# Putting an attention pass between the chunks of a product, layernorms on ScalarE, and a second PSUM bank: a four-layer graph network on one core

## The chip, the cores and the metric

The kernel runs on one core of one Trainium2 chip. The metric is device time in microseconds (us), median of the runs. TensorE is PE in the profiles, VectorE DVE, ScalarE ACT, GpSimd POOL. A "product" below is one matmul call; in fp32 it leaves two instruction records in the trace, so x64 in a profile are 32 calls. A "chunk" is a 1 MB piece of adj or of its transpose as it is loaded, a "block" a group of 512 nodes, a "bank" one of the parts of PSUM, the memory that TensorE writes its sums to.

## The reference, cut to what matters

Four graph layers on N = 4096 nodes with 128 features, each `x = layernorm(x + layer(x))`, all with one 4096 x 4096 matrix `adj`. The change touches the end of the second, the third and the fourth:

```python
# second layer: two Chebyshev convolutions (K = 3) with elu; its last step is one product of adj
# with a 4096 x 128 matrix ("w" below), elu, layernorm
# third layer: attention, 4 heads of 32
C = alpha_src[None, :, :] + alpha_dst[:, None, :]
tau = adj.T[..., None] * exp(maximum(0.2 * C, C))
att = tau / sum(tau, axis=1, keepdims=True)
z = einsum('mnh,nhf->mhf', adj.T[..., None] * att, h_prime)
# fourth layer
out = h @ W_self + (adj @ h / deg) @ W_neigh
```

## The kernel before

The third layer runs in 8 passes (1024 target nodes and 2 of 4 heads each) of 32 steps (128 source nodes each). A step is a vector job with a small product at its end: DVE forms tau, POOL and DVE multiply it once more by the matrix, PE multiplies both into two PSUM banks, `den` and `num`, with 32-column weights.

```python
def attention(mp, hp, between):
    ...
    for nt in range(NT):
        ...                                             # a: chunk of adj; sq = a*a on ScalarE
        for h in range(2):
            nc.vector.scalar_tensor_tensor(tau[:, h, :], D[h], E(h), a, op0=ALU.max, op1=ALU.mult)
        nc.vector.scalar_tensor_tensor(tau2[:, 0, 0:OWN], D[0][:, 0:OWN], E(0), sq, ...)
        nc.gpsimd.tensor_tensor(tau2[:, 0, OWN:WB], tau[:, 0, OWN:WB], a[:, OWN:WB], ALU.mult)
        nc.gpsimd.tensor_tensor(tau2[:, 1, :], tau[:, 1, :], a, ALU.mult)
        product(den, nt, tau, True)
        ...                                             # product(num, ...) of the step before
        between()                                       # one product of the fourth layer
```

After each second pass two blocks of x are complete: their layernorm and the fourth layer's weights follow ("layer-4 block"), and the fourth layer's product with adj runs in pieces in the next two passes ("left-over product"; its last quarter is all that runs after pass 8). Before all this stands the last product of the second layer, whose blocks feed the passes:

```python
for ib, blk, p in propagate(lambda jt: w[:, jt, :], extra=extra):   # 8 blocks of 32 products + wd @ hT, the part that needs no adj
    oT = l1w.tile([P, IB], F32, name="t2T")
    elu(oT, p, B1B)
    ...                                            # transpose, add to x, layernorm
    sources_and_targets(ib)                        # scores: cs, es, hc (sources), dv (targets)
...
def layer3_product(mp):                            # the left-over product
    for ib in range(NB):
        ...
        if mp == 0:
            nc.scalar.copy(acc3[:, blk], p)
        else:
            nc.vector.tensor_add(acc3[:, blk], p, acc3[:, blk])
```

## Time and profile before

Median 2413.23 us (four runs, 2413.23 to 2418.12); the profiled run's span is 2412.5.

| stage | us |
|---|---|
| second layer, last product but one ("v") | 241 |
| second layer, last product | 254 |
| from its end to pass 1 | 20 |
| pass 1, pass 2 | 105, 107 |
| pass 3, pass 4 | 141, 110 |
| pass 5, 6, 7, 8 | 119, 110, 121, 109 |
| left-over product after pass 8 | 94 |

Second part of the profile page, three of its lines: busy share in tenths in 40 equal slices of the span, about 60 us each.

```profile
PE   4899999999999999999999878889888999999987
...
DVE  4433458776011010000222299998799999899965
...
POOL 0000000000000000000000089988798899799940
```

Digits 11 to 23 (most of the second layer) are 8 or 9 on PE and 0 to 2 on DVE; from digit 24 DVE and POOL are busy. Work of the second kind could lie beside work of the first: that is the intent of the change. Its windows by stage stand in the prediction.

### The profile page before, as it was taken

How to read it: one execution, taken by the hardware profiler on the slowest of the kernel's cores; microseconds unless marked ns; L12 is line 12 of the kernel's file. 1: busy time of each engine (PE TensorE's matmuls, PEld its weight loads, DVE VectorE, ACT ScalarE, POOL GpSimd, SP SyncE). 2: the span in 40 equal slices, each digit the busy share in tenths (PEclk: the TensorE clock that was granted, in tenths of full speed). 3: DMA queues.
4: the chain of work that ended last, by engine and by line, in shares of the span. 5: the costliest groups of instructions: out<-in, count | busy, mean ns of one | idle time of the engine just before them, and what ended most of it. 6: DMA issues, size and time to landing. Idle time of an engine off the chain costs nothing. (4 is left out here: it accounts for less than half of the span.)

```text
span 2412.5 us, 23257 instructions
## 1 busy us (share of the span) xinstructions
PE 2252.8 (93%) x8798; PEld 863.4 (36%) x8798; DVE 1366.3 (57%) x2011; ACT 463.3 (19%) x660; POOL 840.4 (35%) x542
## 2 busy tenths in 40 slices
PE   4899999999999999999999878889888999999987
PEld 2334444444444444444444411112222222222233
DVE  4433458776011010000222299998799999899965
ACT  5665000000000000000111122222222222222210
POOL 0000000000000000000000089988798899799940
PEclk8899999999999999999999989999999999999999
DMA  9988788999877878888888735546665666566655
GB/s 361 347 277 261 244 244 259 294 293 291 265 234 244 263 238 278 277 277 276 261 266 264 244 120 160 157 140 209 209 207 194 210 215 239 192 226 232 228 178 168
DMA packets 261802, 575.39 MB, mean 239 GB/s; under 512 B 9776, under 2 KB 15920, under 8 KB 261680
## 3 DMA queue, kind: packets, MB, share of 16 engines
q1 hardware_dynamic: 252352, 566.27, 72.8%
q10 hardware_dynamic: 9328, 7.54, 1.0%
q8 instruction: 71, 1.16, 0.2%
q14 instruction: 51, 0.42, 0.0%
HBM read 571.67 MB, written 2.10 MB: 238 GB/s over the span
## 5 line engine op out<-in xcount | busy, mean ns | idle before, releaser
L624 DVE SCALAR_TENSOR_TENSOR tau<-d,es,chunk 128x1024 f32<-128x1024 f32 x512 | 632.8, 1275 | 28.8 <-issue 18.4
L628 POOL TENSOR_TENSOR tau<-tau,chunk 128x1024 f32<-128x1024 f32 x256 | 606.3, 2368 | 39.0 <-DVE tau L624 31.7
L608 PE MATMUL num<-tau,hc 128*32 128x512 f32 x2048 | 448.1, 602 | 44.6 <-POOL tau L628 42.7
L557 POOL TENSOR_TENSOR x<-x,B2R 128x512 f32<-128x512 f32 x8 | 10.1, 1268 | 1375.8 <-PE ptr L104 1375.8
L608 PE MATMUL den<-tau,cs 128*32 128x512 f32 x2048 | 482.7, 604 | 6.6 <-DVE tau L624 6.1
L619 ACT ACTIVATE sq<-chunk 128x704 f32<-128x704 f32 x256 | 201.8, 792 | 571.3 <-DVE tau L625 568.2
L676 PE MATMUL pp<-chunk,xT 128*128 128x512 f32 x512 | 270.9, 631 | 18.1 <-DMA chunk<-in_adjT 17.2
L313 PE MATMUL pacc<-chunk,hw 128*128 128x512 f32 x512 | 254.6, 635 | 3.0 <-DVE hw L346 3.0
L627 POOL TENSOR_TENSOR tau<-tau,chunk 128x320 f32<-128x320 f32 x256 | 222.2, 868 | 66.0 <-DVE tau L624 20.9
L625 DVE SCALAR_TENSOR_TENSOR tau<-d,es,sq 128x704 f32<-128x704 f32 x256 | 241.0, 941 | 6.3 <-PE num L608 2.5
L444 PE MATMUL pacc<-chunk,w 128*128 128x512 f32 x512 | 226.7, 592 | 0.0
L444 PE MATMUL pacc<-chunk,t 128*128 128x512 f32 x512 | 223.6, 592 | 0.0
L444 PE MATMUL pacc<-chunk,x 128*128 128x512 f32 x512 | 223.5, 594 | 0.0
L444 PE MATMUL pacc<-chunk,v 128*128 128x512 f32 x512 | 221.4, 592 | 0.0
L608 PEld LDWEIGHTS num<-tau,hc 128*32 128x32 f32 x2048 | 83.6, 108 | 291.3 <-POOL tau L628 126.2
L608 PEld LDWEIGHTS den<-tau,cs 128*32 128x32 f32 x2048 | 93.0, 108 | 212.9 <-DVE tau L624 98.8
L293 DVE TENSOR_SCALAR pos<-chunk 128x2048 bf16<-128x2048 f32 x92 | 110.7, 1221 | 75.0 <-DMA chunk<-in_adjT 70.7
L676 PEld LDWEIGHTS pp<-chunk,xT 128*128 128x128 f32 x512 | 82.2, 189 | 198.4 <-issue 165.3
L444 PEld LDWEIGHTS pacc<-chunk,v 128*128 128x128 f32 x512 | 96.6, 190 | 118.1 <-issue 118.1
L444 PEld LDWEIGHTS pacc<-chunk,t 128*128 128x128 f32 x512 | 96.1, 190 | 114.8 <-issue 114.8
L444 PEld LDWEIGHTS pacc<-chunk,x 128*128 128x128 f32 x512 | 95.9, 190 | 113.9 <-issue 113.8
L444 PEld LDWEIGHTS pacc<-chunk,w 128*128 128x128 f32 x512 | 94.9, 190 | 110.3 <-issue 110.3
(161 smaller groups left out, 1321.4 us busy)
## 6 DMA issues: line engine op xcount, KB each, us to landing
chunk<-in_adjT SPq DMA_DIRECT2D x412, 1024.0 KB, 5.5
chunk<-in_adj SPq DMA_DIRECT2D x128, 1024.0 KB, 5.4
xT<-in_xT ACTq DMA_DIRECT2D x8, 256.0 KB, 6.6
out<-o ACTq DMA_DIRECT2D x8, 256.0 KB, 4.0
W1A<-in_w1a ACTq DMA_DIRECT2D x1, 384.0 KB, 8.0
W1B<-in_w1b ACTq DMA_DIRECT2D x1, 384.0 KB, 9.9
W0T<-in_w0gT ACTq DMA_DIRECT2D x1, 64.0 KB, 4.3
W<-in_w0g ACTq DMA_DIRECT2D x1, 64.0 KB, 7.1
```

What stands on the lines that cost most here:

```text
L293: nc.vector.tensor_scalar(pos, a, 0.0, None, op0=ALU.is_gt)
L313: nc.tensor.matmul(p, hw[:, j * TB + k, :], a[:, k, :], start=first and k == 0, stop=last and k == TB - 1)
L444: nc.tensor.matmul(p, stationary(c * TB + k), a[:, k, :], start=n == 0 and k == 0, stop=n == NB - 1 and k == TB - 1 and not more)
L557: nc.gpsimd.tensor_tensor(x[:, tb, :], x[:, tb, :], B2R[:, None, :].to_broadcast([P, TB, F]), ALU.add)
L608: nc.tensor.matmul(acc[q:q + 32, :], weights(nt, 2 * hp + h, is_den), r[:, h, mb * IB:(mb + 1) * IB], start=nt == 0, stop=nt == NT - 1)
L619: nc.scalar.activation(sq, a[:, 0:OWN], AF.Square)
L624: nc.vector.scalar_tensor_tensor(tau[:, h, :], D[h], E(h), a, op0=ALU.max, op1=ALU.mult)
L625: nc.vector.scalar_tensor_tensor(tau2[:, 0, 0:OWN], D[0][:, 0:OWN], E(0), sq, op0=ALU.max, op1=ALU.mult)
L627: nc.gpsimd.tensor_tensor(tau2[:, 0, OWN:WB], tau[:, 0, OWN:WB], a[:, OWN:WB], ALU.mult)
L628: nc.gpsimd.tensor_tensor(tau2[:, 1, :], tau[:, 1, :], a, ALU.mult)
L676: nc.tensor.matmul(p, y[:, (2 * mp + c) * TB + k, :], a[:, k, :], start=c == 0 and k == 0, stop=c == 1 and k == TB - 1)
```

## The change

Four parts. (1) The product of wd with hT leaves the last product for the one before it, and the result (h0T) is added back by VectorE; this frees hT's memory. (2) Pass 1 becomes a generator, and 28 of its 32 steps are issued between the chunks of the last product (6, 5, 5, 4, 4, 4 in blocks 2 to 7), 4 after it. (3) The layer-4 layernorm is done by ScalarE and the residual goes into its weight matrix (+ identity), so that ScalarE copies it. (4) In the last quarter of the left-over product, blocks alternate between two PSUM banks. Core of the diff, cuts marked:

```diff
+    nc.gpsimd.tensor_tensor(W3[:, 1, :], W3[:, 1, :], ident, ALU.add)
...
+            if on_act:
+                nc.scalar.activation(r[:, k, :], r[:, k, :], AF.Identity, bias=m[:, k:k + 1], scale=s[:, k:k + 1])
...
-                    nc.vector.tensor_add(x[:, two, :], q[:, :, 1, :], x[:, two, :])
+                    nc.scalar.copy(x[:, two, :], q[:, :, 1, :])
...
-                    p = ps_p.tile([P, IB], F32, name="pp")
+                    last = mp == NW - 1
+                    p = (ps_nd.tile([P, IB], F32, name="num") if last and ib % 2 else ps_p.tile([P, IB], F32, name="pp"))
...
+                first_pass = attention(l2a, 2, 0, 0)
+                ready = done = 0
+                for ib in range(NB):
+                    p = ps_p.tile([P, IB], F32, name="pp")
+                    for c in range(NB):
+                        a = chunk(ld, adjT, ib, c)
+                        ...                                       # 4 products
+                        if ib >= 2 and done < ready and (c % 2 or ready - done > TB):
+                            next(first_pass)
+                            done += 1
+                    oT = l1w.tile([P, IB], F32, name="t2T")
+                    nc.vector.tensor_add(oT, p, h0T[:, blk])
+                    elu(oT, oT, B1B)
+                    ...
+                    ready += TB
+                for _ in first_pass:
+                    pass
```

Smaller parts: W1A and W1B are loaded later, the squares have two buffers instead of three, and in the last pass x is added on VectorE.

More of the change, by code (lines that the diff above doesn't have):

```diff
@@ L66, in adj_resnorm_d4 @@
         nc.scalar.dma_start(xT[:, g * IB:(g + 1) * IB], xT_in[:, g * IB:(g + 1) * IB])
-    W1A = load_const(w1a.rearrange("k p f -> p k f"), [P, 3, HID], "W1A")
     B1A = load_const(b1a, [P, HH], "B1A")
-    W1B = load_const(w1b.rearrange("k (h p) f -> p (k h) f", p=P), [P, 3 * HH, F], "W1B")
     B1B = load_const(b1b, [P, 1], "B1B")
@@ L110, in stats, with normalize @@
         nc.vector.bn_aggr(mv[:, t, :], st)
-    def normalize(r, g):
+    def normalize(r, g, on_act=False):
+        tb = slice(g * TB, (g + 1) * TB)
         s = small.tile([P, TB], F32, name="rstd")
-        nc.vector.tensor_scalar_add(s, mv[:, g * TB:(g + 1) * TB, 1], LN_EPS)
+        nc.vector.tensor_scalar_add(s, mv[:, tb, 1], LN_EPS)
         nc.scalar.activation(s, s, AF.Sqrt)
         nc.vector.reciprocal(s, s)
+        if on_act:
+            m = small.tile([P, TB], F32, name="mean")
+            nc.vector.scalar_tensor_tensor(m, mv[:, tb, 0], -1.0, s, op0=ALU.mult, op1=ALU.mult)
         for k in range(TB):
-            nc.vector.tensor_scalar(r[:, k, :], r[:, k, :], mv[:, g * TB + k, 0:1], s[:, k:k + 1],
-                                    op0=ALU.subtract, op1=ALU.mult)
+            if on_act:
+                nc.scalar.activation(r[:, k, :], r[:, k, :], AF.Identity, bias=m[:, k:k + 1], scale=s[:, k:k + 1])
+            else:
+                nc.vector.tensor_scalar(r[:, k, :], r[:, k, :], mv[:, g * TB + k, 0:1], s[:, k:k + 1],
+                                        op0=ALU.subtract, op1=ALU.mult)
     def normalize_x(g, pool, name):
@@ L411, in network @@
             l1_pools = ExitStack()
-            with ExitStack() as first:
+            with ExitStack() as first, ExitStack() as l1h_pool:
                 ps_acc, ps_tr, ps_mm = [first.enter_context(tc.tile_pool(name=n, bufs=2, space=PSUM, reuse_waits="tile"))
@@ L421, in network @@
                 dv = state.tile([96, N], BF16, name="dv")
+                selD = state.tile([96, H, P], BF16, name="selD")
                 l1 = l1_pools.enter_context(tc.tile_pool(name="l1", bufs=1, reuse_waits="tile"))
                 l1w = l1_pools.enter_context(tc.tile_pool(name="l1w", bufs=2, reuse_waits="tile"))
+                l1h = l1h_pool.enter_context(tc.tile_pool(name="l1h", bufs=1, reuse_waits="tile"))
+                W1A = l1h.tile([P, 3, HID], F32, name="W1A")
+                nc.scalar.dma_start(W1A, w1a.rearrange("k p f -> p k f"))
+                W1B = l1h.tile([P, 3 * HH, F], F32, name="W1B")
+                nc.scalar.dma_start(W1B, w1b.rearrange("k (h p) f -> p (k h) f", p=P))
                 def elu(dst, p, bias):
@@ L431, in elu, with propagate @@
                     nc.vector.scalar_tensor_tensor(dst, n, -1.0, r, op0=ALU.add, op1=ALU.add)
-                def propagate(stationary, order=range(NB), look=None, extra=None):
+                def propagate(stationary, order=range(NB), look=None):
                     for ib in range(NB):
                         p = ps_acc.tile([P, IB], F32, name="pacc")
-                        more = extra(ib) if extra else []
                         for n, c in enumerate(order):
@@ L444, in propagate @@
                                 nc.tensor.matmul(p, stationary(c * TB + k), a[:, k, :], start=n == 0 and k == 0,
-                                                 stop=n == NB - 1 and k == TB - 1 and not more)
-                        for n, (wgt, r) in enumerate(more):
-                            nc.tensor.matmul(p, wgt, r, start=False, stop=n == len(more) - 1)
+                                                 stop=n == NB - 1 and k == TB - 1)
                         yield ib, slice(ib * IB, (ib + 1) * IB), p
                 t1 = state.tile([P, NT, F], F32, name="t1", tag="yn")
-                t1T = l1.tile([P, N], F32, name="t1T")
-                hT = l1.tile([P, HH, N], F32, name="hT")
-                wd = l1.tile([P, HH, F], F32, name="wd")
+                t1T = l1.tile([P, N], F32, name="t1T", tag="t1T")
+                hT = l1h.tile([P, HH, N], F32, name="hT")
+                wd = l1h.tile([P, HH, F], F32, name="wd")
                 nc.vector.tensor_sub(wd, W1B[:, 0:HH, :], W1B[:, 2 * HH:3 * HH, :])
-                w2x = l1.tile([P, HH, F], F32, name="w2x")
+                w2x = l1h.tile([P, HH, F], F32, name="w2x")
                 nc.vector.tensor_scalar_mul(w2x, W1B[:, 2 * HH:3 * HH, :], 2.0)
-                dsum = l1.tile([P, IB], F32, name="dsum")
+                dsum = l1h.tile([P, IB], F32, name="dsum")
                 def degree(a, first_one):
-                    s = l1w.tile([P, 2, IB], F32, name="dhalf", bufs=1)
+                    s = l1h.tile([P, 2, IB], F32, name="dhalf")
                     nc.vector.tensor_add(s, a[:, 0:2, :], a[:, 2:4, :])
@@ L497, in network @@
                 w = state.tile([P, NT, F], F32, name="w", tag="yn")
+                h0T = l1.tile([P, N], F32, name="h0T", tag="t1T")
                 for ib, blk, p in propagate(lambda jt: v[:, jt, :]):
@@ L507, in network @@
                     nc.vector.tensor_copy(w[:, ib * TB:(ib + 1) * TB, :], q)
-                hc = state.tile([P, NT, H, FO], F32, name="hc", tag="v")
-                att = l1.tile([P, 2, H], F32, name="att")
-                nc.vector.memset(att, 0.0)
-                for h in range(H):
-                    hp = slice(h * FO, (h + 1) * FO)
-                    nc.vector.tensor_copy(att[hp, 0, h:h + 1], ATS[hp, :])
-                    nc.vector.tensor_copy(att[hp, 1, h:h + 1], ATD[hp, :])
-                WD = l1.tile([P, 96], F32, name="WD")
@@ L523, in network @@
-                nc.vector.memset(WD, 0.0)
-                pw = ps_mm.tile([P, 2, H], F32, name="pmm")
-                nc.tensor.matmul(pw, W2, att.rearrange("p s h -> p (s h)"), start=True, stop=True)
-                nc.vector.tensor_copy(W2S[:, F:F + H], pw[:, 0, :])
-                for part in range(3):
-                    nc.vector.tensor_copy(WD[:, 32 * part:32 * part + H], pw[:, 1, :])
-                def sources_and_targets(ib):
-                    blk = slice(ib * IB, (ib + 1) * IB)
-                    for half in range(2):
-                        two = slice(ib * TB + 2 * half, ib * TB + 2 * half + 2)
-                        pn = ps_mm.tile([P, 2, F + H], F32, name="pmm")
-                        for k in range(2):
-                            t = ib * TB + 2 * half + k
-                            nc.tensor.matmul(pn[:, k, :], xT[:, t * P:(t + 1) * P], W2S, start=True, stop=True)
-                        nc.scalar.activation(cs[:, two, :], pn[:, :, F:F + H], AF.Exp, scale=0.2)
-                        nc.scalar.activation(es[:, two, :], pn[:, :, F:F + H], AF.Exp, scale=0.8)
-                        for k in range(2):
-                            t = ib * TB + 2 * half + k
-                            nc.vector.tensor_mul(hc[:, t], pn[:, k, 0:F].rearrange("p (h f) -> p h f", f=FO),
-                                                 cs[:, t, :][:, :, None].to_broadcast([P, H, FO]))
-                    pd = ps_mm.tile([96, IB], F32, name="pmm")
-                    nc.tensor.matmul(pd, WD, xT[:, blk], start=True, stop=True)
-                    d = l1w.tile([96, IB], F32, name="elu_r")
-                    nc.scalar.activation(d, pd, AF.Exp, scale=-0.8)
-                    nc.vector.tensor_copy(dv[:, blk], d)
-                    nc.vector.tensor_sub(d, d, dv[:, blk])
-                    nc.vector.tensor_copy(dv[32:64, blk], d[32:64, :])
-                    nc.vector.tensor_copy(dv[64:96, blk], d[64:96, :])
-                    nc.vector.tensor_sub(d[64:96, :], d[64:96, :], dv[64:96, blk])
-                    nc.vector.tensor_copy(dv[64:96, blk], d[64:96, :])
-                    tb = slice(ib * TB, (ib + 1) * TB)
-                    nc.gpsimd.tensor_tensor(x[:, tb, :], x[:, tb, :], B2R[:, None, :].to_broadcast([P, TB, F]), ALU.add)
@@ L559, in network @@
-                extra = lambda ib: [(wd[:, hh, :], hT[:, hh, ib * IB:(ib + 1) * IB]) for hh in range(HH)]
-                for ib, blk, p in propagate(lambda jt: w[:, jt, :], extra=extra):
-                    oT = l1w.tile([P, IB], F32, name="t2T")
-                    elu(oT, p, B1B)
-                    q = transpose4(ps_tr, "ptr", lambda k: oT[:, k * P:(k + 1) * P])
-                    xb = x[:, ib * TB:(ib + 1) * TB, :]
-                    nc.vector.tensor_add(xb, q, xb)
-                    for t in range(ib * TB, (ib + 1) * TB):
-                        stats(x[:, t, :], t)
-                    normalize_x(ib, ps_tr, "ptr")
-                    sources_and_targets(ib)
@@ L570, in network @@
-            l1_pools.close()
+                    ph = ps_mm.tile([P, IB], F32, name="pmm")
+                    for hh in range(HH):
+                        nc.tensor.matmul(ph, wd[:, hh, :], hT[:, hh, blk], start=hh == 0, stop=hh == HH - 1)
+                    nc.scalar.copy(h0T[:, blk], ph)
             ps_d = enter(name="ps_d", bufs=1, space=PSUM)
@@ L579, in network @@
             ps_x = enter(name="ps_x", bufs=1, space=PSUM)
-            l2w = enter(name="l2w", bufs=1)
-            selD = l2w.tile([96, H, P], BF16, name="selD")
-            rows = l2w.tile([96, H], F32, name="rows")
+            hc = state.tile([P, NT, H, FO], F32, name="hc", tag="v")
+            y = xT.rearrange("p (t f) -> p t f", f=F)
+            att = l1.tile([P, 2, H], F32, name="att")
+            nc.vector.memset(att, 0.0)
+            for h in range(H):
+                hp = slice(h * FO, (h + 1) * FO)
+                nc.vector.tensor_copy(att[hp, 0, h:h + 1], ATS[hp, :])
+                nc.vector.tensor_copy(att[hp, 1, h:h + 1], ATD[hp, :])
@@ L583, in network @@
+            WD = l1.tile([P, 96], F32, name="WD")
+            nc.vector.memset(WD, 0.0)
+            pw = ps_x.tile([P, 2, H], F32, name="px")
+            nc.tensor.matmul(pw, W2, att.rearrange("p s h -> p (s h)"), start=True, stop=True)
+            nc.vector.tensor_copy(W2S[:, F:F + H], pw[:, 0, :])
+            for part in range(3):
+                nc.vector.tensor_copy(WD[:, 32 * part:32 * part + H], pw[:, 1, :])
+            rows = small.tile([96, H], F32, name="rows")
             nc.vector.tensor_reduce(rows, ident[0:96, :].rearrange("p (q c) -> p c q", q=4)[:, 0:H, 0:3], AX.X, ALU.add)
@@ L584, in network, with sources_and_targets @@
             nc.vector.tensor_copy(selD, rows[:, :, None].to_broadcast([96, H, P]))
-            acc3 = state.tile([P, N], F32, name="acc3", tag="yn")
-            y = xT.rearrange("p (t f) -> p t f", f=F)
+            def sources_and_targets(ib):
+                blk = slice(ib * IB, (ib + 1) * IB)
+                for half in range(2):
+                    two = slice(ib * TB + 2 * half, ib * TB + 2 * half + 2)
+                    pn = ps_x.tile([P, 2, F + H], F32, name="px")
+                    for k in range(2):
+                        t = ib * TB + 2 * half + k
+                        nc.tensor.matmul(pn[:, k, :], xT[:, t * P:(t + 1) * P], W2S, start=True, stop=True)
+                    nc.scalar.activation(cs[:, two, :], pn[:, :, F:F + H], AF.Exp, scale=0.2)
+                    nc.scalar.activation(es[:, two, :], pn[:, :, F:F + H], AF.Exp, scale=0.8)
+                    for k in range(2):
+                        t = ib * TB + 2 * half + k
+                        nc.vector.tensor_mul(hc[:, t], pn[:, k, 0:F].rearrange("p (h f) -> p h f", f=FO),
+                                             cs[:, t, :][:, :, None].to_broadcast([P, H, FO]))
+                pd = ps_x.tile([96, IB], F32, name="px")
+                nc.tensor.matmul(pd, WD, xT[:, blk], start=True, stop=True)
+                d = l1w.tile([96, IB], F32, name="elu_r")
+                nc.scalar.activation(d, pd, AF.Exp, scale=-0.8)
+                nc.vector.tensor_copy(dv[:, blk], d)
+                nc.vector.tensor_sub(d, d, dv[:, blk])
+                nc.vector.tensor_copy(dv[32:64, blk], d[32:64, :])
+                nc.vector.tensor_copy(dv[64:96, blk], d[64:96, :])
+                nc.vector.tensor_sub(d[64:96, :], d[64:96, :], dv[64:96, blk])
+                nc.vector.tensor_copy(dv[64:96, blk], d[64:96, :])
+                tb = slice(ib * TB, (ib + 1) * TB)
+                nc.gpsimd.tensor_tensor(x[:, tb, :], x[:, tb, :], B2R[:, None, :].to_broadcast([P, TB, F]), ALU.add)
@@ L588, in weights, with attention @@
             def weights(nt, head, den):
                 return cs[:, nt, head:head + 1].to_broadcast([P, FO]) if den else hc[:, nt, head, :]
-            def attention(mp, hp, between):
+            def attention(l2w, bufs, mp, hp):
                 D = []
@@ L617, in attention @@
                     a = a2t[:, nt % 2, :]
-                    sq = l2w.tile([P, OWN], F32, name="sq", bufs=3)
+                    sq = l2w.tile([P, OWN], F32, name="sq", bufs=2)
                     nc.scalar.activation(sq, a[:, 0:OWN], AF.Square)
-                    tau = l2w.tile([P, 2, WB], F32, name="tau", bufs=3)
-                    tau2 = l2w.tile([P, 2, WB], F32, name="tau2", bufs=3)
+                    tau = l2w.tile([P, 2, WB], F32, name="tau", bufs=bufs)
+                    tau2 = l2w.tile([P, 2, WB], F32, name="tau2", bufs=bufs)
                     E = lambda h: es[:, nt, 2 * hp + h:2 * hp + h + 1]
@@ L632, in attention @@
                         product(num, *late.pop(0), False)
-                    between()
+                    yield
                 product(num, *late.pop(0), False)
@@ L647, in attention @@
                     xb = xb.rearrange("p k (h f) -> p k h f", f=FO)
-                    nc.gpsimd.tensor_tensor(xb, z[:, :, :, mb, :], xb, ALU.add)
+                    eng = nc.vector if mp == NW - 1 and hp == 1 else nc.gpsimd
+                    eng.tensor_tensor(xb, z[:, :, :, mb, :], xb, ALU.add)
             def layer3_block(j):
@@ L654, in layer3_block @@
                     stats(x[:, t, :], t)
-                normalize(x[:, tb, :], j)
+                normalize(x[:, tb, :], j, on_act=True)
                 q = transpose4(ps_x, "px", lambda k: x[:, j * TB + k, :])
@@ L685, in layer3_product @@
                         nc.vector.tensor_add(acc3[:, blk], p, acc3[:, blk])
-                    if mp == NW - 1:
+                    if last:
                         layer3_out(ib)
@@ L699, in layer3_out @@
                 nc.scalar.dma_start(out[ib * IB:(ib + 1) * IB, :].rearrange("(k p) f -> p k f", p=P), o)
+            with tc.tile_pool(name="l2a", bufs=1, reuse_waits="tile") as l2a:
+                first_pass = attention(l2a, 2, 0, 0)
+                ready = done = 0
+                for ib in range(NB):
+                    blk = slice(ib * IB, (ib + 1) * IB)
+                    tb = slice(ib * TB, (ib + 1) * TB)
+                    p = ps_p.tile([P, IB], F32, name="pp")
+                    for c in range(NB):
+                        a = chunk(ld, adjT, ib, c)
+                        for k in range(TB):
+                            nc.tensor.matmul(p, w[:, c * TB + k, :], a[:, k, :], start=c == 0 and k == 0,
+                                             stop=c == NB - 1 and k == TB - 1)
+                        if ib >= 2 and done < ready and (c % 2 or ready - done > TB):
[4 more added lines that the diff above has]
+                    elu(oT, oT, B1B)
+                    q = transpose4(ps_x, "px", lambda k: oT[:, k * P:(k + 1) * P])
+                    nc.vector.tensor_add(x[:, tb, :], q, x[:, tb, :])
+                    for t in range(ib * TB, (ib + 1) * TB):
+                        stats(x[:, t, :], t)
+                    normalize_x(ib, ps_x, "px")
+                    sources_and_targets(ib)
+                    ready += TB
+                for _ in first_pass:
+                    pass
+            l1_pools.close()
+            l2w = enter(name="l2w", bufs=1)
+            acc3 = state.tile([P, N], F32, name="acc3", tag="yn")
             pieces = iter(())
@@ L703, in network @@
                 for hp in range(H // 2):
-                    attention(mp, hp, lambda: next(pieces, None))
+                    if (mp, hp) != (0, 0):
+                        for _ in attention(l2w, 3, mp, hp):
+                            next(pieces, None)
                 for _ in pieces:
```

## The prediction

> **What bounds the kernel now.** I read the stage windows first, then the page's groups, then the chain of waits. The windows (stretch, then busy us per engine, granted clock, DMA share, GB/s) cut the part that the change touches at its stage ends: the second layer's last product, its tail, the eight passes of the third layer, the left-over product.
>
> ```profile
> core 0: us, PE busy (x) PEld busy (x) DVE busy (x) ACT busy (x) POOL busy (x), PEclk, DMA share, GB/s
> 1122.00:1376.60 254.60, 254.60 (x695) 119.01 (x694) 62.31 (x194) 40.16 (x78) 8.87 (x7) 1.00 0.86 266
> 1376.60:1395.30 18.70, 7.04 (x21) 3.55 (x19) 9.43 (x29) 7.80 (x14) 1.27 (x1) 0.63 0.20 67
> 1395.30:1500.60 105.30, 88.65 (x509) 16.84 (x510) 103.83 (x96) 24.58 (x32) 101.08 (x64) 0.97 0.48 150
> 1500.60:1607.30 106.70, 89.14 (x525) 17.13 (x524) 104.78 (x98) 26.36 (x34) 103.59 (x67) 1.00 0.51 158
> 1607.30:1748.30 141.00, 127.37 (x627) 32.89 (x627) 114.72 (x130) 31.98 (x48) 104.44 (x67) 0.98 0.57 194
> 1858.10:1977.40 119.30, 114.56 (x613) 30.80 (x612) 114.19 (x134) 29.25 (x42) 103.89 (x67) 1.00 0.60 206
> 1977.40:2087.80 110.40, 107.97 (x589) 27.09 (x590) 107.57 (x103) 26.45 (x35) 104.01 (x67) 1.00 0.67 229
> 2087.80:2208.90 121.10, 116.36 (x613) 31.25 (x612) 113.72 (x135) 29.33 (x43) 104.07 (x67) 0.99 0.60 208
> 2344.00:2402.00 58.00, 52.67 (x140) 23.44 (x140) 30.68 (x134) 1.44 (x7) 0.00 (x0) 1.00 0.61 195
> ```
>
> The last product is PE's alone: 254.60 of 254.60 us, DVE a quarter busy. The first pass is the reverse: DVE 103.83 of 105.30, POOL 101.08 close behind. So the two stages want different engines, and that is the idea. Pass 3 is 35 us longer than pass 1, passes 5 and 7 some 10 us longer than 6.
>
> ```profile
> L624 DVE SCALAR_TENSOR_TENSOR tau<-d,es,chunk 128x1024 f32<-128x1024 f32 x512 | 632.8, 1275 | 28.8 <-issue 18.4
> L625 DVE SCALAR_TENSOR_TENSOR tau<-d,es,sq 128x704 f32<-128x704 f32 x256 | 241.0, 941 | 6.3 <-PE num L608 2.5
> L628 POOL TENSOR_TENSOR tau<-tau,chunk 128x1024 f32<-128x1024 f32 x256 | 606.3, 2368 | 39.0 <-DVE tau L624 31.7
> L608 PE MATMUL num<-tau,hc 128*32 128x512 f32 x2048 | 448.1, 602 | 44.6 <-POOL tau L628 42.7
> L608 PE MATMUL den<-tau,cs 128*32 128x512 f32 x2048 | 482.7, 604 | 6.6 <-DVE tau L624 6.1
> L444 PE MATMUL pacc<-chunk,w 128*128 128x512 f32 x512 | 226.7, 592 | 0.0
> ```
>
> A step (256 in all, 32 a pass) is two L624 and one L625; in the timeline of passes 1 and 2 the steps follow each other every 3.24 us, and 32 x 3.24 = 104. POOL's two instructions take 2.37 + 0.87 = 3.24 as well.
>
> From the chain of waits (start, us, what):
>
> ```profile
> 1677.82 5.31 DMA chunk<-in_adjT
> 1691.32 5.75 DMA chunk<-in_adjT
> ...
> 1952.65 1.92 PE pp L676 x4
> 1955.56 1.06 PE pp L676 x2
> ...
> 2378.36 6.88 PE pp L676 x16
> 2386.66 6.88 PE pp L676 x16
> ```
>
> Late in pass 3 (and into 4) whole chunk loads lie on the chain, one every 13 to 15 us: the timeline shows 12 of them going in turn into one and the same buffer, each waiting for the last chunk's final matmul. In the left-over product a block is 6.88 us of matmul, but the next begins 8.31 later: 1.43 us for emptying the one PSUM bank.
>
> **What the Trainium skill says.** "TensorEngine Tiling (Array Packing)", Key Properties: changing the tiling mode drains TensorE. The trace agrees: 16 equal products take 6.88 (0.86 a pair), a lone pair between 32-column products 1.06, so 0.20 a switch. "Perfetto Trace Analysis", Identifying the Most-Contended Engine: matmul busy share misleads, as matmuls are pipelined. Agrees: pass 6 shows PE 107.97 of 110.40, yet DVE's 107.57 sets the pace, and PE's weight loads are 27. "VectorE: DVE Perf Modes", Side-by-side: fp32 two-tensor operations get no faster mode; L624's 1275 ns for 1024 elements agrees, so nothing shrinks DVE's step. "ScalarE: Activation LUTs", What ACT_TABLE_LOAD costs: an ACTIVATE is about 280 ns plus 0.83 per element, about 93 more for each pointer operand. My estimate for the moved normalise is then 0.28 + 128 x 0.83 ns + 0.09, near 0.45 us, as dear as on DVE; no instruction of this kind is in the trace.
>
> **The change part by part.**
>
> 1. The product of wd with hT (a pair per call and block, 8 x 1.71 = 13.7 us of PE at 0.857 a call pair) moves from the last product into the one before it, also PE-bound: +13.7 there, -13.7 here, plus one 0.7 us add per block on DVE, idle there.
>
> 2. The interleave. In the changed program's order of instructions, 28 of the 32 steps stand in the last product: 6, 5, 5, 4, 4, 4 in blocks 2 to 7, and 4 after it. What a step costs PE: a group of 4 narrow products alone advances PE 0.98 us, 4 den and 4 num together 1.85 (from starts in the timeline of pass 8, 2276.17 to 2278.02), plus 0.20 for the switch: 2.05. So PE's sum is 254.6 - 13.7 + 28 x 2.05 = 298.3. DVE has 28 x 3.24 + 62 = 153 and POOL about 100 of those 298: no longer bounds. To this I add stalls by judgement: 1.4 us in each of blocks 0 and 1 (the bank is single now; from the third block on, the order puts steps' products ahead of the transposes, which hides it), 3.6, 3.7, 2.6 in blocks 2 to 4 and 2.5 in each of the last three, where a step's products wait for POOL in PE's queue: 20. The stage becomes 318. After it: the block's chain of elu, layernorm and scores 11.7 (of 18.7 today), 4 steps 13, the last quotient 3, some 1 for starting pass 2: 28.7. Together 347. Today the same is 254.6 + 18.7 + 105.3 + 0.5 = 379.1. Gain 32, less part 1's 13.7: **-18.3**. So 94 us of pass hidden cost 57 of PE and 20 of stalls.
>
> 3. Weights W1A and W1B are no longer loaded at the start, which is bound by DMA (768 KB near 380 GB/s: -2), but late in layer 0, where the second layer's first vector work waits for them: +3. **+1**.
>
> 4. Pass 2 has two buffers fewer for the squares and new ones for tau: **+1**.
>
> 5. Layernorms on ScalarE. For a pair of blocks DVE loses 8 x 0.445 (L119 in pass 5) = 3.6, 4 adds of 0.42 = 1.7, and 1.5 of waits for ACT: 6.8 us, at DVE's price because the pass is DVE's. ACT has 75 us spare per pass, but its squares (one a step) stand in the same queue behind the chain, so I count two thirds: -4.5 for each of passes 5 and 7: **-9**. In pass 3 the same, and the order has 10 loads in a row into one buffer in place of 12: **-8** for passes 3 and 4.
>
> 6. Two banks in the left-over product: 7 gaps of 1.43, of which about 1.0 goes (the narrow transposes stay between blocks), and 1 for the x add of the last pass on DVE: **-8**.
>
> Sum: -18.3 + 1 + 1 - 9 - 8 - 8 = -41.3; 2413.2 - 41.3 = 2371.9.
>
> **The rivals.**
>
> A. TensorE becomes the bound and gives the hidden time back. PE executes in order, and a den or num that waits for DVE or POOL holds up the product's matmuls behind it. For it: L608 waits for POOL already, 42.7 us in all; each of blocks 2 to 7 would lose 5 us more, and with the four steps after the end slower, the gain of part 2 goes: near 2400. Against it: products run one step late, and in the merged stage DVE and POOL have twice the time per step.
>
> B. Chunk loads set the pace of passes 3 and 4 whatever DVE does. For it: the DMA lines above, each load 5.3 to 5.8 us. Then part 5's -8 is 0, or worse where the ring of buffers falls otherwise; ScalarE's chain may also delay the squares, as there are 2 buffers for them. 2380 to 2390.
>
> C. The stalls of part 2 are smaller than my 20 us. For it: PE's busy time is modelled, DVE and POOL are far from full, and the order hides the evacuations. With 5 us of stalls and part 5 in full: near 2345.
>
> D. The merged stage becomes DMA's. Against it: 266 GB/s today; 64 chunks plus 14 MB in 318 us are about 256 GB/s. I give it no weight.
>
> **Range and chances.** The one large judged term is the stalls (20, could be 5 to 35), then the passes (-17, could be -25 to 0). Rival A and B together reach 2400, C 2345. Predicted 2372, 8 in 10 between 2348 and 2397. Faster by over 2% needs under 2365: 0.36. Within 2%: 0.62. Slower by 2% needs over 2461: no sum comes near; 0.02.
>
> **What would show it.** Part 2: the stretch from the last product's start to pass 2's first step 347 us with PE over 95% busy up to the product's end; blocks 0 and 1 near 31.5, block 2 near 46, the last three near 41. If blocks 5 to 7 are near 45 and PE waits for tau, A is right; near 38.5, C. Part 1: the product before is longer by 13 to 14. Part 5: no L119-like work on DVE in passes 5 and 7, which take near 115; if they stay at 120, ScalarE's chain is the cause. Pass 3 near 135 with chunk loads still on the chain; if unchanged, B. Part 6: block starts 7.2 to 7.4 us apart in the left-over product; if 8.3, the bank was not the cause. The whole is wrong if the gain stands elsewhere than in part 2's stage and the left-over product.

## The result, and the profile after

Median 2379.57 us (four runs, 2378.07 to 2384.19) against 2413.23: ratio 0.9859, 95% interval 0.984 to 0.9878. A ratio is the mean time of one kernel's fast runs over that of the other's of the same rounds, so not quite the ratio of the medians. In the profiled runs the span fell from 2412.5 to 2376.4, 36.1 us. By stage (starts of passes are the starts of their first tau instruction, ends of products those of their last matmul, and pass 8 ends with the end of its last tau instruction):

| stage | before | after | difference | predicted |
|---|---|---|---|---|
| up to the start of "v" | 880.9 | 879.1 | -1.8 | +1 |
| "v", last product, up to pass 2 | 620.2 | 609.4 | -10.8 | -18 |
| pass 2 | 106.8 | 104.8 | -2.0 | +1 |
| passes 3 and 4 | 250.7 | 237.3 | -13.4 | -8 |
| passes 5 and 7 | 240.4 | 238.3 | -2.1 | -9 |
| passes 6 and 8 | 218.9 | 218.9 | 0.0 | 0 |
| after pass 8 | 94.5 | 88.5 | -6.0 | -8 |

The windows of the changed kernel (stretch, then busy us of PE, PEld, DVE, ACT, POOL with instructions, clock, DMA share, GB/s): last product, from its end to pass 2, passes 3 to 7, the left-over product:

```profile
1137.00:1452.20 315.20, 311.97 (x1071) 120.56 (x1075) 168.20 (x284) 63.33 (x108) 104.30 (x63) 0.99 0.77 253
1452.20:1488.50 36.30, 26.50 (x119) 7.55 (x118) 25.35 (x42) 9.69 (x17) 14.91 (x9) 0.76 0.31 109
...
1593.30:1722.40 129.10, 120.35 (x630) 31.66 (x634) 108.77 (x121) 36.27 (x61) 103.89 (x67) 0.99 0.62 212
1722.40:1830.60 108.20, 96.88 (x574) 25.21 (x566) 105.26 (x99) 28.23 (x39) 102.86 (x66) 1.00 0.65 214
1830.60:1950.50 119.90, 115.36 (x612) 31.27 (x612) 111.68 (x125) 33.22 (x55) 103.94 (x67) 0.99 0.61 207
1950.50:2060.90 110.40, 107.91 (x588) 27.11 (x588) 107.56 (x103) 26.41 (x35) 104.23 (x67) 1.00 0.66 229
2060.90:2179.30 118.40, 113.83 (x612) 31.14 (x612) 111.64 (x125) 33.36 (x55) 104.08 (x67) 1.00 0.63 213
2310.20:2366.00 55.80, 55.64 (x149) 24.62 (x147) 30.97 (x134) 2.08 (x9) 0.00 (x0) 1.00 0.69 222
```

The first row is the merged stage: PE is still busy throughout, now with DVE at 168 and POOL at 104 of 315 beside it. It is 61 us longer than the last product was (254.6). The second row is what is left of pass 1, 36 us with every engine partly idle. Pass 5 is no shorter than before, though DVE's busy time fell from 114.19 to 111.68. And in pass 3 PE has 630 instructions, in pass 4 only 574, where passes 5 and 6 have 612 and 588: keep that in mind. (The kernel before has nearly the same numbers, 627 in pass 3 by the prediction's table, so this is not a result of the change.)

One line of the changed kernel's DVE timeline, in pass 5, shows a new wait (start, us, what, in brackets the idle time and its releaser):

```profile
1869.61 0.69 DVE L686 TENSOR_TENSOR acc<-pp,acc 128x512 f32<-128x512 f32 x1 [3.97 <-PE pp L677]
```

DVE waits for the left-over product; in pass 5 of the kernel before it never did. PE had no gap of 0.3 us or more in the 14 us before: it was working off a backlog from the layer-4 block.

Two lines each of the DVE timeline and of the POOL timeline of the changed kernel:

```profile
1286.43 2.88 DVE L443 SCALAR_TENSOR_TENSOR t2T<-elu_n,elu_r 128x512 f32<-128x512 f32 x1
...
1472.40 2.48 DVE L581 CAST dv<-elu_r 32x512 bf16<-32x512 f32 x1
```
```profile
1286.41 2.34 POOL L627 TENSOR_TENSOR tau<-tau,chunk 128x1024 f32<-128x1024 f32 x1
...
1472.02 2.58 POOL L627 TENSOR_TENSOR tau<-tau,chunk 128x1024 f32<-128x1024 f32 x1 [0.55 <-DVE tau L623]
```

The same instructions take 0.69 and 0.42 us in the other blocks. Each of the long ones starts just after a POOL multiply and ends with it plus its own time: 2.88 is about 2.34 + 0.69 less some overlap. "SBUF — State Buffer" of the Trainium skill, Who interferes with whom, states this: VectorE and GpSimd share a port pair under an exclusive lock, for VectorE's operations with two SBUF inputs (against a GpSimd instruction that reads SBUF, as the multiply does) and for copies and casts in their fast modes, and "Issue order, not op shape, decides who blocks." Here the trace agrees, and an experiment below shows the other order.

### The profile page after: what moved, and what is told of

The parts are those of the page before. It is cut to its first block, busy times and chain, and to the rows that moved or that the text cites. A ratio compares the mean times of both kernels' runs of the same rounds, so it can differ in the third digit from the quotient of the medians.

```text
span 2376.4 us, 23290 instructions
## 1 busy us (share of the span) xinstructions
PE 2247.5 (95%) x8798; PEld 860.8 (36%) x8798; DVE 1371.0 (58%) x1981; ACT 484.2 (20%) x716; POOL 847.5 (36%) x541
## 4 chain that ended last, share of the span: by engine, by line
PE 83%; DVE 9%; DMA 4%; issue 2%; ACT 1%; POOL 1%; DVEq 0%; ACTq 0%; POOLq 0%
PE pacc L455 27%; PE pacc L319 10%; PE den L607 10%; PE pp L677 10%; PE pp L712 10%; PE num L607 7%; DVE tau L623 5%; DMA chunk<-in_adjT 3%; PE pmm L496 2%; PE num L677 1%; PE px L103 1%; PE pden L305 1%; DVE tau L624 1%; PE ptr L314 1%; PE px L663 1%
## 5 line engine op out<-in xcount | busy, mean ns | idle before, releaser
L607 PE MATMUL den<-tau,cs 128*32 128x512 f32 x2048 | 457.5, 605 | 8.6 <-DVE tau L623 8.1
L607 PE MATMUL num<-tau,hc 128*32 128x512 f32 x2048 | 413.8, 601 | 32.1 <-POOL tau L627 27.6
L677 PE MATMUL pp<-chunk,xT 128*128 128x512 f32 x448 | 243.5, 637 | 11.8 <-DMA chunk<-in_adjT 11.4
L712 PE MATMUL pp<-chunk,w 128*128 128x512 f32 x512 | 235.6, 602 | 1.2 <-DVE t2T L718 1.2
L607 PEld LDWEIGHTS den<-tau,cs 128*32 128x32 f32 x2048 | 86.0, 108 | 222.3 <-issue 106.0
L517 DVE COPY w<-ptr 128x512 f32<-128x512 f32 x8 | 5.5, 692 | 246.1 <-PE ptr L515 246.1
L712 PEld LDWEIGHTS pp<-chunk,w 128*128 128x128 f32 x512 | 92.2, 190 | 124.6 <-issue 117.7
```

The source lines that it names most:

```text
L607: nc.tensor.matmul(acc[q:q + 32, :], weights(nt, 2 * hp + h, is_den), r[:, h, mb * IB:(mb + 1) * IB], start=nt == 0, stop=nt == NT - 1)
L677: nc.tensor.matmul(p, y[:, (2 * mp + c) * TB + k, :], a[:, k, :], start=c == 0 and k == 0, stop=c == 1 and k == TB - 1)
L712: nc.tensor.matmul(p, w[:, c * TB + k, :], a[:, k, :], start=c == 0 and k == 0, stop=c == NB - 1 and k == TB - 1)
```

## The experiments

Twelve kernels, in three groups, each on one chip; every one gave a correct result. The times are given as medians, and as ratios to the kernel before on the same chip; differences between two kernels are those of the ratios times 2413 us. A ratio's interval is about 0.002 either way, 5 us, that of the difference of two some 7, so a difference of a few us is read from the stage in the trace, not from the total.

### e1_not_between: pass 1 whole, after the product

```diff
-                        if ib >= 2 and done < ready and (c % 2 or ready - done > TB):
+                        if False:
```

> The changed kernel, but all 32 steps of the first pass come after the last product (none between its chunks). Theory (hiding is paid for in TensorE time: a step costs the product 2.06 us of PE plus extra time at block ends, and saves 3.24 us of DVE): the product shrinks from 315 to about 245 us, the stretch from its end to the second pass's first step grows from 36 to about 121, so 351 becomes 366 and the kernel about 15 us slower, near 2394. Rival A (the interleave gives everything back): within 5 us of the changed kernel, 2375 to 2385. Rival C (hiding is nearly free): 30 us or more slower, over 2409.

2390.52 us, ratio 0.9910: 12 us slower than the changed kernel. Its windows for the product and for the stretch up to pass 2:

```profile
1136.50:1383.00 246.50, 241.81 (x649) 110.26 (x651) 74.09 (x206) 43.42 (x82) 16.14 (x11) 1.00 0.84 264
1383.00:1499.70 116.70, 97.19 (x542) 20.53 (x542) 111.81 (x120) 30.20 (x43) 98.47 (x61) 0.99 0.48 158
```

So the interleave adds 315.2 - 246.5 = 68.7 us to the product and takes 116.7 - 36.3 = 80.4 from what follows. It gains 11.7 us and costs 68.7 for 28 steps, 2.45 us a step, of the 3.24 that a step takes alone. Where nothing disturbs it (8 products, or 16 records, and then a step), a step advances PE by 8.91 - 6.85 = 2.06 us; the rest of the 2.45 is at block ends. The theory is right, at 12 us for its 15; both rivals are out.

### e2_norm_on_vector: layernorm and residual add of the layer-4 block back on VectorE

```diff
-                normalize(x[:, tb, :], j, on_act=True)
+                normalize(x[:, tb, :], j)
...
-                    nc.scalar.copy(x[:, two, :], q[:, :, 1, :])
+                    nc.vector.tensor_add(x[:, two, :], q[:, :, 1, :], x[:, two, :])
```
(and the identity taken out of the weights)

> The changed kernel with the layer-4 layernorm and the residual add back on VectorE (weights without the identity). Theory (in passes 5 and 7 TensorE's backlog took the place of DVE, so the move gained little there, and pass 3's gain is partly the order of chunk loads): passes 5 and 7 change by 0 to +2 us each, pass 3 by +3 to +6, the start of the tail by 1: total +4 to +9, 2384 to 2389. Rival P (the prediction's part 5): 13 to 17 us slower, 2393 to 2397. Rival N (the move is worth nothing): within 2 us.

2392.88 us, ratio 0.9906: 11 us slower, between theory and rival. By stage: pass 3 139.9 in place of 129.1, pass 4 +2.3, pass 5 +1.1, pass 7 +2.6. So in passes 5 and 7 the move is worth about as little as the theory had it, but in pass 3 it is worth 11 us, more than either said. Why pass 3 is different had to be found.

### e3_one_bank: one PSUM bank in the left-over product

```diff
-                    p = (ps_nd.tile([P, IB], F32, name="num") if last and ib % 2 else ps_p.tile([P, IB], F32, name="pp"))
+                    p = ps_p.tile([P, IB], F32, name="pp")
```

> The changed kernel with a single PSUM bank in the left-over product. Theory: the pitch of its blocks goes from 7.45 back to 8.31 us, 7 x 0.86 = 6 us slower, near 2385.6. Rival: something else (the x add on DVE) makes the tail shorter, and the time stays within 2 us of 2379.6.

2386.46 us, ratio 0.9884: 6 us slower. The chains of waits (start, us, what), first of the changed kernel with two banks, then of this one:

```profile
2315.15 6.01 PE num L677 x14
2321.16 0.86 PE pp L677 x2
2322.02 0.58 PE px L103 x4
2322.60 6.01 PE pp L677 x14
```
```profile
2326.75 6.88 PE pp L677 x16
2333.63 0.02 issue
2333.65 0.70 DVE acc L686
2334.36 0.04 issue
2334.40 0.66 PE px L103 x4
2335.06 6.88 PE pp L677 x16
```

With two banks a block's pitch is 7.45 us and PE never stops; with one it is 8.31, and the add that empties the bank lies on the chain. Seven blocks of 0.86 are 6.0.

### e4_casts_on_scalar: the four bf16 casts of dv on ScalarE

```diff
-                nc.vector.tensor_copy(dv[:, blk], d)
+                nc.scalar.copy(dv[:, blk], d)
```
(likewise the other three)

> The changed kernel with the four bf16 casts of each block's dv on ScalarE instead of DVE. In the changed kernel the casts took up to 2.48 us instead of 0.42 where GpSimd's multiply ran at the same time. Theory (they lie on the path after the product's end, on DVE, 3.7 us there): the stretch from the product's end to the second pass's first step goes from 36.3 to 32 or 33, the kernel 3 to 4 us faster, near 2376. Rival 1 (in the product they also hold up the steps and through them TensorE): 6 us or more faster. Rival 2 (the chain after the end is set by the scores and POOL, not by these): within 1 us.

2372.90 us, ratio 0.9833: 6 us faster, as rival 1 had it, but not for its reason. The stretch after the product became 33.9 instead of 36.3 (theory: 32 to 33), and the product 311.4 instead of 315.2. That 3.8 is not the casts' doing: it is the one elu instruction of block 3, on the DVE and POOL timelines of this kernel:

```profile
1286.09 0.68 DVE L443 SCALAR_TENSOR_TENSOR t2T<-elu_n,elu_r 128x512 f32<-128x512 f32 x1
```
```profile
1286.08 2.91 POOL L627 TENSOR_TENSOR tau<-tau,chunk 128x1024 f32<-128x1024 f32 x1
```

In the changed kernel the POOL record starts 0.02 us ahead of it and DVE took 2.88; here it starts 0.01 us ahead, but DVE took its 0.68 and POOL's record grew to 2.91, so DVE was first in effect. Block 4 was 45.8 us from first product to first product before and 41.96 here. A kernel with the casts left on DVE (e7 below) also had 311.4, and its eight elu instructions all took 0.69 or less. So this is a matter of some hundredths of a us in the order of issue, not of the casts as such.

### e6_multiply_on_vector: POOL idle in the interleaved steps

```diff
+                    multiply = nc.vector if bufs == 2 and nt < 28 else nc.gpsimd
-                    nc.gpsimd.tensor_tensor(tau2[:, 0, OWN:WB], tau[:, 0, OWN:WB], a[:, OWN:WB], ALU.mult)
+                    multiply.tensor_tensor(tau2[:, 0, OWN:WB], tau[:, 0, OWN:WB], a[:, OWN:WB], ALU.mult)
```
(and the second multiply likewise)

> The changed kernel with GpSimd's two multiplies of the 28 interleaved steps on VectorE (about 1.2 + 0.4 us a step more there, 45 in all, while DVE is half idle); the four steps after the end as before. Theory (VectorE's casts, and one elu and the mean, are held up while GpSimd multiplies): with GpSimd idle there, every cast in the product takes 0.42 us and the product is 3 to 5 us shorter (315 to 311), as with the casts on ScalarE; 2375 to 2377. Rival 1 (the load of DVE delays the block's chain and the steps): product 3 us or more longer. Rival 2 (the long casts have nothing to do with GpSimd): casts stay at 0.8 to 1.6 us.

2388.73 us, ratio 0.9900. The cause is confirmed, the gain is not. In the changed kernel the first and second of the four casts took 0.77 and 1.6 us in blocks 2 to 6; here every cast of blocks 0 to 6 takes 0.42 and every elu 0.69, and only in block 7, after the product, where POOL multiplies again, two are longer, 0.68 and 2.47. That falls to theory and against rival 2. But the product is 322.1 us, 6.9 longer: DVE's 199 us of work there delay the steps and the block's chain, as rival 1 said. POOL's share is worth its lock.

### e5_own_buffers and e9_before_own_buffers: buffers of their own for the left-over product's chunks

Both kernels had a run of 11 to 13 loads of the left-over product into one and the same buffer in passes 3 and 4. From pass 2 on:

```diff
+            ld_pool.close()
+            ld = enter(name="lda", bufs=4)
+            ldT = enter(name="ldt", bufs=2)
...
-                        a = chunk(ld, adjT, ib, 2 * mp + c)
+                        a = chunk(ldT, adjT, ib, 2 * mp + c)
```

> The changed kernel, but from the second pass on the chunks of the left-over product have two buffers of their own and the passes' chunks four (before: six for both; in the changed kernel 11 of the left-over product's loads in a row go into one and the same buffer). Theory (that run of loads is what still stretches pass 3): pass 3 goes from 129 to 117 to 120 us, pass 4 from 108 to 107, no chunk load on the chain of waits there; 9 to 12 us faster, 2368 to 2371. Rival (the order of loads only shows where PE or DVE is late anyway, or four buffers are too few for the passes): within 3 us of 2379.6, or slower.

> The kernel before with the same own buffers (two and four) after the second layer, nothing else. Theory (13 loads in a row into one buffer make pass 3 long): pass 3 from 141 to 118 to 123 us, pass 4 from 110 to 107, the kernel 20 to 25 us faster, 2388 to 2393, so that a good part of what the change gained in pass 3 comes from where its loads happen to fall. Rival (DVE's layer-4 block and its waits make pass 3 long): less than 10 us faster.

2404.27 us, ratio 0.9959, and 2431.35, ratio 1.0071: both slower than without. My theory fell. Part of it is the stretch after pass 8 (105 us in place of 88.5 in e5, where PE waits 6.4 us for chunks: two buffers seem too few for a product that runs alone). But no chunk load was left on the chain in pass 3 of e5, and still pass 3 grew, from 129.1 to 134.0 (in e9 from 141.0 to 149.0). The windows of e5 for passes 3 and 4 show the reason:

```profile
1595.70:1729.70 134.00, 130.00 (x648) 32.77 (x652) 108.85 (x121) 37.09 (x63) 103.93 (x67) 0.99 0.63 213
1729.70:1838.70 109.00, 98.09 (x556) 21.45 (x548) 104.93 (x99) 27.24 (x37) 103.21 (x66) 1.00 0.61 202
```

PE has 648 instructions in pass 3 and 556 in pass 4. Counted by kind, pass 3 holds 96 records of the left-over product and pass 4 holds 32: 48 products and 16 of 64. In the changed kernel, and in the kernel before, it is 39 and 25, in e9 52 and 12, in passes 5 and 6 of the kernels up to here 32 and 32. The source asks for one product a step, which would be 32 and 32 everywhere; but the program that is built has another order, as the traces show (products, `den` and `num` of different steps alternate on PE). That order puts the first of these products too early, and in pass 3 the products then sit in PE's queue ahead of steps that DVE waits for; pass 4, which DVE holds at 105 us, gains nothing from having fewer.

### e7_own_buffers_norm_vector: e5 and e2 together

> As the kernel with own buffers, and the layernorm and residual add back on VectorE. Alone, that move back cost 11 us, nearly all in pass 3, and the run of loads into one buffer grew from 11 to 13 with it. Theory (most of those 11 us were that run, not VectorE's work): against the kernel with own buffers 3 to 6 us slower, pass 3 by 2 to 3. Rival (VectorE's work and waits at the start of pass 3): still 9 to 12 us slower.

2414.62 us, ratio 1.0007, 12 us slower than e5: the rival's number. But in it pass 3 alone is 150.6 us, 16.6 longer, and the crowding has grown with it (52 and 12 products), so it does not tell whether VectorE's work is dear by itself or only in a crowded pass.

### e10_sum_on_vector: the first product's blocks copied out by VectorE

Why only passes 3 and 4? The first left-over product differs from the later ones in one line: its blocks leave PSUM by a ScalarE copy, the others by a VectorE add that stands in DVE's order among the steps. That this is what the build goes by is inferred from the code; what the traces show is that the order changes with the line.

```diff
-                        nc.scalar.copy(acc3[:, blk], p)
+                        nc.vector.tensor_copy(acc3[:, blk], p)
```

> The changed kernel with one line other: the first left-over product's blocks are copied out of PSUM by VectorE instead of ScalarE (8 copies of 0.69 us). The order of the built program then has 32 of the 64 product instructions in pass 3 and 32 in pass 4 (39 and 25 before), and no run of loads into one buffer. Theory S (with ScalarE emptying the bank nothing in DVE's order held the product back, so too much of it was ordered into pass 3, where TensorE then sets the pace, and pass 4 cannot be shorter than DVE's 105): pass 3 from 129 to 119 to 121 as pass 5, pass 4 from 108 to 110.4 as pass 6; 7 us faster, near 2373. Rival (the copies cost DVE what is gained): within 2 us of 2379.6.

2368.87 us, ratio 0.9811 (0.9791 to 0.9831): 11.6 us faster than the changed kernel and the fastest of all. Its windows for passes 3 and 4:

```profile
1591.80:1709.70 117.90, 113.22 (x612) 30.21 (x612) 110.16 (x125) 34.56 (x57) 104.00 (x67) 0.99 0.61 211
1709.70:1820.00 110.30, 107.91 (x588) 27.11 (x588) 107.50 (x102) 26.30 (x35) 104.09 (x67) 1.00 0.66 228
```

612 and 588 instructions as in passes 5 and 6, and 117.9 and 110.3 us. Eight more copies on the engine that bounds the pass made it 11 us shorter; pass 4 is 2 longer, so that 9 of the gain lie in these two. No chunk load lies on the chain in passes 3 and 4 any more: with the order, the run of loads into one buffer went too. What PE waited in pass 3 stands in the view of waits (us in total, times, longest), for the kernel before and for the changed one:

```profile
PE pp L676 <- DMA chunk<-in_adjT: 8.9, 5, 2.5
```
```profile
PE pp L677 <- DMA chunk<-in_adjT: 4.7, 3, 2.0
```

In e5, e10 and e12 there is no such wait, and in none of these pass 3s does PE wait for ScalarE to empty the bank, so the copy's own delay is not the cause. How much is which: a lone product between steps takes 1.06 us. The changed kernel's pass 3 has 7 too many, 7.4 us, and 4.7 of waits: 12.1, measured 11.2. The kernel before, 7.4 and 8.9: 16.3, measured 141.0 - 125.1 (e12) = 15.9. From the changed kernel to e5, 4.7 less and 9 products more, 9.5: +4.8, measured +4.9. So the loads did cost something, and e5 hid it by making the order worse; for e9 the same sum falls 3 us short. These are estimates from the traces; no run took the waits away alone.

### e11_sum_and_norm_on_vector: e10 and e2 together

> As the last one, and the layer-4 layernorm and residual add back on VectorE. Theory S (most of the 11 us that this cost alone came from the crowded pass 3): 3 to 6 us slower than the last one, 1 to 2 in each of passes 3, 5 and 7. Rival (it is VectorE's own work at the start of pass 3): 9 to 12 us slower than the last one.

2376.33 us, ratio 0.9835: by the ratios 6 us slower than e10, by the medians 7.5. In the traces pass 3 is 125.2 in place of 117.9, pass 5 +1.1, pass 7 +2.8. So by the ratios about half of e2's loss came from the crowded pass, as the theory has it. But in pass 3 itself 7.3 of 10.8 us remain, more than the 1 to 2 expected. The trace shows where: in pass 3 one normalise takes 2.37 us instead of 0.34, beside a GpSimd multiply, and VectorE's adds wait 6.4 us for ScalarE's copies of the same banks; in pass 5 it is 1.21 and 1.9, in pass 7 0.34 and 4.2. The passes stand in the same order as their losses; no run took these apart.

### e12_before_sum_on_vector: the same one line in the kernel before

> The kernel before with the same one line (first product copied out by VectorE); its order too goes from 39 and 25 to 32 and 32. Theory S: passes 3 and 4 from 251 to 230 to 233 together, 18 to 21 us faster, 2392 to 2395, so that the change itself is worth about 20 us and not 34 once both have it. Rival (DVE's waits in the layer-4 block make pass 3 long): less than 8 us faster.

2397.22 us, ratio 0.9924: 18 us faster than the kernel before, with one line. Passes 3 and 4 take 125.1 and 110.4 us, 235.5 in place of 250.7 (expected 230 to 233). With the line in both, the change is worth 0.9811 / 0.9924 = 0.9886, 27 us, not the 20 that I expected.

### e13_spread: no products at the start of the odd passes

e10 with e4's casts, and:

```diff
-                        for _ in attention(l2w, 3, mp, hp):
-                            next(pieces, None)
+                        for n, _ in enumerate(attention(l2w, 3, mp, hp)):
+                            if hp or n >= 8:
+                                next(pieces, None)
+                            if hp and n % 4 == 3:
+                                next(pieces, None)
```

> The changed kernel with the copy on VectorE, the casts on ScalarE (alone 6.7 us), and in passes 3, 5 and 7 no product instruction in the first 8 steps, in passes 4, 6 and 8 an extra one every fourth step (24 and 40 in place of 32 and 32). Theory (the start of the odd passes is TensorE's: layer-4 block, steps and products together fall behind, and DVE then waits for the product): odd passes 3 to 5 us shorter, even ones 0 to 3 longer; about 2380 - 7 - 6.7 - 5 = 2361. Rival (the start of the odd passes is set by the layer-4 chain on ScalarE and DVE; the even passes pay the extra): no gain or a loss from the spreading, 2366 or more.

2376.43 us, ratio 0.9839: slower than e10. The odd passes did become shorter, 344.7 us together instead of 354.6, so their start was PE's. But the even ones took 345.9 instead of 329.3, and what follows pass 8 another 5 us. At the end of pass 4, on this kernel's DVE timeline:

```profile
1823.88 1.28 DVE L623 SCALAR_TENSOR_TENSOR tau<-d,es,chunk 128x1024 f32<-128x1024 f32 x1 [4.32 <-PE d L597]
```

DVE, done with pass 4, waits 4.32 us for the first PE instruction of the next pass, which stands behind the backlog. The even passes had no room on PE for the moved products, though DVE set their pace.

## Why the prediction was right, point by point

The time came out at 2379.6 for 2372 predicted, inside the range, and the outcome is "within 2%", the likeliest of the three. The sum is right partly by luck, because errors cancel: parts 2, 5 (passes 5 and 7) and 6 fell short by 7.5, 6.9 and 2.0 us, and passes 3 and 4 and parts 3 and 4 gave 5.4, 2.8 and 3.0 more than counted. One of its own signs went against it: "the whole is wrong if the gain stands elsewhere than in part 2's stage and the left-over product". Only 16.8 of the 36.1 us stand there. (Its own sum, with 17 us in the passes, did not fit that sign either.)

- Part 1, wd moved (+13.7): right. "v" went from 241.3 to 253.3 us by its products, for seven of the eight blocks, and 4.5 us more pass before the last product starts (none before), in which PE does the last block's transposes and products.
- Part 2, the product: right. From the start of "v" to the end of the last product the time grew by 573.1 - 495.0 = 78.1 us; the prediction says 13.7 + (318 - 254.6) = 77. Its cost of a step, 2.05 us on PE, was measured at 2.06, and the 20 us of stalls were 16.6 (315.2 less 219.4 for the 256 products, 57.7 for the steps, and 21.5 of block ends that the kernel before had too). The last three blocks took 41.0, 41.0 and 39.2 us, near the 41 named. But the size was right for a wrong reason: PE's waits in the stage come to 3.2 us in all, for VectorE (2.0 of them for the elu that POOL held up), and none for POOL. Most of the 16.6 is time in which PE works: by a count of its order in the trace the 28 steps come in 44 groups, cut up at the block ends, and each change from narrow to wide products costs some 0.2 us. So rival A holds in its first half, though not by its waits: TensorE is the bound, and hiding 28 steps costs 69 of the 80 us gained (e1). Its second half, that nothing is left, is wrong.
- Part 2, after the product: the mis-sized term is "4 steps 13". Measured: 10.4 us to the first step (predicted 11.7), 21.1 for the four steps, 4.8 to pass 2 (predicted 4). Among the four steps DVE does the last block's dv, 5.1 us, of which 2.1 are one cast held up by POOL; I had left that work out. Of the other 3 us, 2.1 are waits for ScalarE's exponentials of the scores. That makes the stage's gain 10.8 and not 18.3.
- Part 5, passes 5 and 7 (-9, measured -2.1): the step that failed is "6.8 us, at DVE's price because the pass is DVE's". At the start of the odd passes PE is behind (the line at 1869.61 above), and e13 shows these passes shorten when PE has less to do. The sign named for this case, "ScalarE's chain is the cause", holds only for 2.0 us, PE's wait for a normalise on ScalarE in pass 5. Nor did PE have the room that the prediction read into pass 6, where it took the busy share of 107.97 of 110.40 us to mislead: 8 products more there, about 8.5 us at 1.06, made the pass 7 us longer in e13. A smaller error: the 0.445 for one normalise was a mean with one long instruction in it; seven of the eight took 0.34, the other 1.21. On ScalarE one takes 0.48 to 0.49 us; the prediction's own terms, summed right (0.28 + 0.11 + 0.09), give 0.48, not the "near 0.45" written. (In "ScalarE: Activation LUTs", What ACT_TABLE_LOAD costs, the 280 ns already hold one pointer operand, the bias; the 93 are for the second, the scale.)
- Part 5, passes 3 and 4 (-8, measured -13.4): both its terms were right in kind and too small. The layernorm and the add were counted at 4.5; with the order repaired in both kernels they are worth 7.3 us in pass 3 (e10 and e11). The rest, 3.5, was for the order of loads; PE's waits for chunks fell from 8.9 to 4.7 us in pass 3 and from 8.2 to 6.6 in pass 4, 5.8 together. So rival B was right in part. What neither saw is what made pass 3 long in both kernels: products ordered too early onto PE (e10, e12). As this is the same before and after, it gave no gain here.
- Part 6, two banks (-8, measured -6.0): the bank's share was 0.86 a block, not 1.0, and no gain from the x add shows. e3 confirms the mechanism at 6 us.
- Parts 3 and 4 (+1 each) were -1.8 and -2.0: no cost where I had allowed one. Neither was tried alone.
- Rival C is out: the stalls were near 17 us. Rival D: 253 GB/s in the merged stage for 256 estimated, and the bound is PE.
- Slips that leave the sum alone: the "94 us of pass hidden" come out of its own terms as 96 (124.5 - 28.7), pass 3 is 36 us longer than pass 1 and not 35, and the chunk loads on the chain follow each other every 13.5 to 16.7 us, not every 13 to 15.

## What to carry to other kernels

Work put beside a busy engine is free only for the engines that were idle: count what each hidden step takes from the busy one, here 2.06 of 3.24 us at least, and add the ends of the blocks. When one pass of several alike is slower, compare instruction counts per engine between the passes before anything else: here 630 against 612 pointed to the order of the built program, and one line then gave 9 us in two passes. When an experiment takes a suspected cause away, count again what else it moved: e5 took away 4.7 us of waits for loads and looked like a refutation, because the order got 9 products worse at the same time.

## What the Trainium skill lacked or had wrong

- "TensorEngine Tiling (Array Packing)" says that a change of mode drains TensorE, without a size: here 0.20 us on the product after it (1.06 instead of 0.86 for its pair of records; after a transpose, 128 wide as the products are, it is 0.86), so a step costs 2.06 us of PE in place of 1.85.
- "SBUF — State Buffer" has the lock between VectorE and GpSimd, and the runs agree (casts of 0.42 us took up to 2.48, an elu of 0.69 took 2.88). What it lacks is how this looks in a profile: the instruction's own record grows and no wait is shown, so that a group's mean hides it (0.445 for 0.34), and 0.02 us or less in the order of issue moved a whole stage by 3.8 us.
- No page has it that the choice of the engine which empties PSUM can change how early the built program's order places the products: with a ScalarE copy in place of VectorE's it was 39 and 25 instead of 32 and 32, and passes 3 and 4 took 9.0 us more in the changed kernel and 15.3 in the one before (12 and 18 by the ratios).
